# Self edges taken out of a graph kernel's gathers: the edge list compacted on the chip, each window's own rows loaded plainly

## The chip, the cores and the metric

One of the eight cores of a Trainium2 chip runs the whole kernel. The metric is the device time of one execution in microseconds (us). The engines named below are TensorE (PE, its weight loads PEld), VectorE (DVE), ScalarE (ACT), GpSimd (POOL) and SyncE (SP, which here issues DMA transfers and reads registers). Each executes its own instructions in order and waits on semaphores.

## The reference

A graph of 6250 nodes (256 features) has 106250 edges, sorted by destination. 50000 random pairs are there in both directions, and then every node has one edge to itself: each destination has at least one edge, and 6250 of the 106250 edges are such self edges, each the last of its destination. Every edge has one of 8 types.

```python
h = relu(layernorm(x))
for l in range(3):                       # relational layers
    xr  = einsum('nd,rde->rne', h, W_rel[l])
    agg = segment_sum(xr[edge_type, src], dst)
    h   = relu(agg + h @ W_root[l] + bias[l])
x = x + h
h = relu(layernorm(x)); h = h @ Wv + bv  # attention over the same edges
e = leaky_relu(q(h)[src] + k(h)[dst], 0.2)
out = x + segment_sum(h[src] * softmax_by_dst(e), dst)
```

## The kernel before

**Preparation (L517 to L664).** Sources, destinations (twice, the second shifted by one) and types are loaded 128 edges to a row (load_edges, three DMAs each, SP and ACT), turned by PE so that a chunk of 128 consecutive edges is one column (turned, L548), and DVE derives for each of the 831 chunks the node and the (node, type) segment of each edge relative to a window's first node. DVE also checks that the list is sorted and that each window fits; the flag bad_i (L656) selects ordered_path or a general path for other graphs. No instruction of ordered_path starts before the flag. Then x is normalized and written as a table tab[0] in HBM, each row as three bf16 parts whose sum has float32's precision (L688 to L719).

**Windows.** The chunks are grouped into 57 windows (42 of 15 chunks, 14 of 14, a last one of 5). A window covers at most 128 destination nodes from its first node, base, on. For each chunk k of a window, node_ranges gives the nodes that its edges can hit, a range of 13 to 42 nodes; with 8 types that is 104 to 336 segments.

**A relational layer (L908 to L1007).** The loop runs over all chunks (t, k); engine order is as written (manual_schedule). For each chunk: POOL gathers 128 rows of 1536 bytes of tab[l] by the edges' sources (gather, L733), with 30 buffers; DVE makes a one-hot of edges by segments (make_hot, L921), five chunks ahead; PE multiplies message parts by the one-hot into PSUM banks (add, L953, six matmuls, or twelve where the range crosses the middle of the window; with hot_p, also the last chunk of the window before, whose last node can run over). The first half of the banks is copied to ag by ACT when its last chunk is done, the second at the window's end (evacuate, L841). In layer 0 one chunk of each window comes not from the table but from raw rows of x, gathered at the start (L815) and normalized by norm_split.

**The end of a window (finish, L843).** finish is a generator; the loop takes one step of it per chunk of the *next* window. Step 0 turns the window's own rows (xt, loaded by SP at k=1 of the window itself, L994) by six matmuls (L851). Then the output matmuls: 16 products of ag with W_rel (L866) and two with W_root (L870), spread over steps 1 to 12 (to 10 in the last layer) into one PSUM tile po. Then DVE and ACT in turn add the bias and split the result into three parts (L874, L668 to L671), and SP writes them to tab[l + 1] (L878). In the last layer three steps instead add x, normalize, write xa and hx (L893, L903); hx holds 257 columns, the last being the query term. So SP's order in a layer is: xt of window t, write of window t-1 at its end, xt of window t+1.

**Layer ends.** The next layer's gathers need the whole table, so POOL waits there for the last window's write. Weights have two buffers; the load of layer l+1's is issued by ACT at the start of layer l.

**Attention (L1009 to L1097).** Window by window: a gather of 128 hx rows per chunk, logits masked and turned on DVE, ACT and PE, exponentials, and a weighted sum on PE. A window has 16 operands: its chunks and the last chunk of the window before.

## Time and profile before

| what | us |
|---|---|
| median of 10 runs (lowest, highest) | 4349.46 (4347.14, 4352.2) |
| the profiled execution | 4349.26 |
| its span, first to last instruction | 4347.5 |
| POOL: first raw gather; first gather of layer 1, layer 2, attention | 36.2; 1137.7, 2206.6, 3277.0 |
| PE busy, DVE busy, ACT busy, POOL busy | 3731.8, 2123.5, 1269.6, 3165.8 |
| mean clock granted to PE | 0.959 |

Busy time is what an engine spent executing, not issuing. A line of a group names the source line, the engine, the operation, output <- inputs and the count; behind the bar stand busy time and the mean of one in ns, and then the idle time just before, with what ended it. In a table by stretches the columns are the stretch, its length, then for PE, PEld, DVE, ACT, POOL the busy time with the number of instructions, the granted PE clock, the share of the DMA engines and GB/s. A line of a timeline has the start, the length, the instruction and the number of equal ones merged; a bracket gives idle time before it and what ended it. Two lengths may overlap, so starts are compared. SPq means that SP's sequencer issued it.

### The profile page before, as it was taken

What the parts mean: (1) busy time and instruction counts of PE and PEld (TensorE: products, weight loads), DVE (VectorE), ACT (ScalarE), POOL (GpSimd) and SP (SyncE); (2) the same over time, 40 slices, a digit from 0 to 9 for tenths busy, and PEclk for the clock granted to TensorE, in tenths of its full rate; (3) what the DMA queues carried; (4) which work ended last, traced back from release to release, by engine and by line L of the source; (5) the groups of instructions that cost most, each with busy time, mean ns of one, the idle gap of its engine ahead of it and who ended that gap; (6) DMA issues with size and microseconds to landing.
All of it is one profiled execution on the core that took longest, in us unless ns stands there. A gap on an engine that the chain in (4) does not pass through costs nothing. (4 is left out here: it accounts for less than half of the span.)

```text
span 4347.5 us, 85514 instructions
## 1 busy us (share of the span) xinstructions
PE 3731.8 (86%) x31754; PEld 3152.8 (73%) x31754; DVE 2123.5 (49%) x6301; ACT 1269.6 (29%) x2850; POOL 3165.8 (73%) x3403
## 2 busy tenths in 40 slices
PE   0899999999799999999989999999995777777777
PEld 0688888877677777777767777777774666667666
DVE  6444445444333333333334444444445666666665
ACT  5122222222111111111111111111114556555555
POOL 5777777777477777777757777777766777777775
PEclk9999999999999999999999999999997888888888
DMA  6766666666466666666646666666663444444443
GB/s 225 217 180 180 180 180 183 180 180 178 126 180 181 177 180 181 180 180 181 180 142 191 191 188 190 191 191 191 191 175 99 121 120 121 121 121 118 121 123 93
DMA packets 305229, 720.22 MB, mean 166 GB/s; under 512 B 63333, under 2 KB 159409, under 8 KB 304801
## 3 DMA queue, kind: packets, MB, share of 16 engines
q0 software_dynamic: 198608, 596.13, 48.9%
q1 hardware_dynamic: 95868, 109.36, 7.7%
q10 hardware_dynamic: 10324, 9.18, 0.7%
q8 instruction: 251, 4.11, 0.4%
q14 instruction: 178, 1.45, 0.1%
HBM read 660.18 MB, written 54.26 MB: 164 GB/s over the span
## 5 line engine op out<-in xcount | busy, mean ns | idle before, releaser
L733 POOL DMA_INDIRECT msg<-tab,src_t x2436 | 2309.1, 948 | 821.7 <-issue 363.1
L953 PE MATMUL bank<-hot,msg 128*128 128x104 bf16 (+15 forms) x17304 | 1699.5, 241 | 269.4 <-DMA msg<-tab,src_t 164.2
L953 PEld LDWEIGHTS <-msg 128*128 128x128 bf16 x18312 | 1367.2, 98 | 667.2 <-DMA msg<-tab,src_t 292.0
L866 PE MATMUL po<-wr,ag 128*128 128x256 f32 (+1 forms) x5472 | 1537.0, 393 | 44.8 <-DVE hml L671 33.9
L921 DVE TENSOR_SCALAR hot<-up,seg 128x104 bf16<-128x104 f32 (+12 forms) x2493 | 961.5, 430 | 554.8 <-PE bank L953 548.0
L733 POOL DMA_INDIRECT head<-hx,src_t x831 | 787.5, 948 | 280.6 <-issue 94.8
L866 PEld LDWEIGHTS po<-wr,ag 128*128 128x128 f32 (+1 forms) x5472 | 903.2, 190 | 114.4 <-DVE hml L671 39.3
L841 ACT COPY ag<-bank 128x512 f32<-128x512 f32 x675 | 362.0, 589 | 1755.7 <-PE bank L953 1737.7
L874 DVE TENSOR_TENSOR po<-po,bb 128x256 f32<-128x256 f32 x171 | 74.0, 433 | 1016.5 <-PE po L870 1016.5
L1076 PE MATMUL pf<-ex,head 128*128 128x128 f32 (+1 forms) x3548 | 466.9, 295 | 3.3 <-DVE ex L1073 3.2
L1076 PEld LDWEIGHTS pf<-ex,head 128*128 128x128 f32 x3548 | 456.7, 212 | 11.1 <-DVE ex L1073 5.8
L1046 ACT ACTIVATE qm<-other,head 128x128 f32<-128x128 f32 (+1 forms) x887 | 321.3, 398 | 297.9 <-DMA head<-hx,src_t 161.9
L1048 PE MATMUL pq<-ident,qm 128*128 128x128 f32 (+1 forms) x887 | 184.6, 305 | 121.9 <-ACT qm L1046 116.7
L1038 DVE TENSOR_SCALAR other<-up,loc 128x128 f32<-128x128 f32 x831 | 255.8, 341 | 61.9 <-ACT qm L1046 61.3
L1067 PE MATMUL pe<-ident,c 128*128 128x128 f32 (+1 forms) x887 | 152.7, 314 | 123.4 <-ACT c L1061 71.8
L1048 PEld LDWEIGHTS pq<-ident,qm 128*128 128x128 f32 (+1 forms) x887 | 117.7, 149 | 166.7 <-ACT qm L1046 162.3
L1067 PEld LDWEIGHTS pe<-ident,c 128*128 128x128 f32 (+1 forms) x887 | 116.7, 160 | 147.5 <-ACT c L1061 85.6
L1052 DVE TENSOR_REDUCE tops<-pq 128x1 f32<-128x512 f32 (+1 forms) x226 | 153.0, 677 | 123.8 <-ACT c L1051 123.3
L870 PE MATMUL po<-wo,x_t 128*128 128x256 f32 (+1 forms) x684 | 176.4, 380 | 0.0
L1053 DVE SCALAR_TENSOR_TENSOR c<-pq,k_n,c 128x512 f32<-128x512 f32 (+1 forms) x226 | 165.5, 732 | 0.0
L668 ACT ACTIVATE hml<-po 128x256 bf16<-128x256 f32 (+1 forms) x114 | 44.2, 388 | 389.8 <-DVE po L874 362.5
L1051 ACT ACTIVATE c<-pq,sm 128x512 f32<-128x512 f32 (+1 forms) x226 | 145.7, 672 | 2.2 <-DVE sm L1030 1.4
(159 smaller groups left out, 1787.6 us busy)
## 6 DMA issues: line engine op xcount, KB each, us to landing
msg<-tab,src_t POOLq DMA_INDIRECT x2436
xt<-tab SPq DMA_DIRECT2D x168, 192.0 KB
tab<-hml SPq DMA_DIRECT2D x112, 192.0 KB
head<-hx,src_t POOLq DMA_INDIRECT x831
tab<-hml SPq DMA_DIRECT2D x12, 768.0 KB
hx<-row SPq DMA_DIRECT2D x56, 128.5 KB
x<-in_x_dram SPq DMA_DIRECT2D x56, 128.0 KB
xa<-x SPq DMA_DIRECT2D x56, 128.0 KB
```

Of the source, the lines that this page charges most:

```text
L733: nc.gpsimd.indirect_dma_start(out=to, out_offset=None, in_=table[:N, :], in_offset=bass.IndirectOffsetOnAxis(ap=index, axis=0))
L841: nc.scalar.copy(to, of)
L866: nc.tensor.matmul(po[:m], ag[:, h, r, :m], wr[:, h, r, :], start=(r == 0 and h == 0), stop=False, skip_group_check=True)
L870: nc.tensor.matmul(po[:m], x_t[:, h, :m], wo[:, h, :], start=False, stop=(h == KH - 1), skip_group_check=True)
L921: nc.vector.tensor_scalar(hot[:, :R * (hi - lo)], up[:, :R * (hi - lo)], seg[:, i:i + 1], None, op0=ALU.is_equal)
L953: nc.tensor.matmul(banks[b][h][:, a - b * SEG // 2:z - b * SEG // 2], w, hot[:, a - lo:z - lo], start=(not begun[b] and s_ == 0), stop=Fal ...
L1038: nc.vector.tensor_scalar(other[:, :m], up[:, :m], refs[j][1], None, op0=ALU.not_equal)
L1046: nc.scalar.activation(qm[:, :m], other[:, :m], AF.Identity, scale=MASKED, bias=refs[j][0][:, D:HX])
L1048: nc.tensor.transpose(pq[:m, i, :], qm[:, :m], ident)
L1053: nc.vector.scalar_tensor_tensor(to, flat, k1, to, op0=ALU.add, op1=ALU.max)
L1067: nc.tensor.transpose(pe[:, i, :m], c_t[:m, j * P:(j + 1) * P], ident[:m, :m])
L1076: nc.tensor.matmul(pf[:, h, :m], refs[j][0][:, h * P:(h + 1) * P], ex[:, i, :m], start=(j == 0 and h == 0), stop=(j == len(refs) - 1 and h ...
```

## The change

The self edges leave the gathered lists, and 784 chunks take the place of 831: 57 windows again, 51 of 14 chunks, 5 of 13, one of 5.

- Preparation: edges are loaded in overlapping rows of 193 (34 rows for each 4608 edges, 102 rows at a time, 8 times; seven DMAs for each of three arrays, and three for the first nodes). The last edge of each destination is dropped (its word is zero; that it is the self edge is checked for the flag), and its type is noted with the edge before it. Source, node, type and that note are packed in one integer; six steps shift entries left by 1, 2, 4 ... 32 where that bit of the remaining offset is set, each by a mask (into PSUM), a masked copy and a predicated copy. The fields are unpacked and turned. More checks go into the flag.
- Layers: for each window a row tells for every node the type of its self edge (count_loops, computed in layer 0 one window ahead: a one-hot on DVE, a matmul per chunk, a copy). The window's own rows are loaded at k=0, turned at k=3 (own_rows), and by k=7 eight products (one per type) put the own row under the right type in by. evacuate then adds by to the PSUM banks on DVE instead of copying them on ACT. finish loses its step 0's matmuls; its output matmuls take steps 1 to 11 (1 to 9 in the last layer).
- One-hots are made for two chunks by one instruction (make_hots).
- Buffers: messages 26 for 30, weights 1 for 2 (loaded at the start of their own layer), rows 1 for 2, PSUM banks 4 for 5.
- Attention: each window's own 128 rows of hx come as one transfer on SP (mine) and are a further operand; with that a window has 16 operands again.

```diff
--- before.py
+++ after.py
-CW = 15
+
+CW = 14
 LAST = 5
-SPREAD = 4.5
+SPREAD = 4.25
+GR = 36
+GK = 34
+GP = 3
+STEP = 135
+LEAD = 4
+WIDE = 191
+BITS = 6
+OWN = 1024
...
-    NC = -(-E // P)
-    NB = -(-NC // P)
+    NG = E // (GR * P)
+    REST = E - NG * GR * P
+    KR = -(-math.ceil(REST * (1 - N / E) + 4) // P) if REST else 0
+    NC = NG * GK + KR
+    PB = GP * GK
+    NB = -(-NC // PB)
...
+        def load_edges(name: str, a: bass.AP, front: int, fill: int, eng):
+
+            s = prep.tile([PB, NB, WL], I32, name=name)
+            nc.vector.memset(s[:, 0, :LEAD], front)
+            nc.vector.memset(s[:, LB, :], fill)
+
+            def load(to: bass.AP, g: int, i: int, dims):
+                at = a.offset + g * GR * P + i * STEP - LEAD
+                eng.dma_start(to, bass.AP(tensor=a.tensor, offset=at, ap=dims))
+
+            for h in range(GP):
+                nb = (NG - h + GP - 1) // GP
+                b = 0
+                if h == 0:
+                    eng.dma_start(s[0:1, 0, LEAD:], bass.AP(
+                        tensor=a.tensor, offset=a.offset, ap=[[0, 1], [1, WL - LEAD]]))
+                    load(s[1:GK, 0, :], 0, 1, [[STEP, GK - 1], [1, WL]])
+                    b = 1
+                load(s[h * GK:(h + 1) * GK, b:nb, :], b * GP + h, 0,
+                     [[STEP, GK], [GP * GR * P, nb - b], [1, WL]])
+            for i in range(KR):
+                p = NG % GP * GK + i
+                n = min(WL, REST - i * STEP + LEAD)
+                load(s[p:p + 1, LB, :n], NG, i, [[0, 1], [1, n]])
+            return s
...
+        dst_r = load_edges("dst_r", dst, -1, N, nc.sync)
+        src_r = load_edges("src_r", src, -1, N, nc.scalar)
...
+        word = [prep.tile([PB, NB, WIDE], I32, name=f"word{i}") for i in range(2)]
+        nc.vector.scalar_tensor_tensor(word[0], src_r[:, :, :WIDE], 14, tag,
+                                       op0=ALU.logical_shift_left, op1=ALU.bitwise_or)
...
+            n = WIDE
+            for k in range(BITS):
+                a, z = word[k % 2], word[(k + 1) % 2]
+                m = mps.tile([PB, NB, WIDE + 1], I32, name="m")
+                nc.vector.tensor_scalar(m[:, :, :n], a[:, :, :n], 28 - k, 31,
+                                        op0=ALU.logical_shift_left, op1=ALU.arith_shift_right)
+                n1 = n - (1 << k)
+                nc.vector.scalar_tensor_tensor(z[:, :, :n1], m[:, :, :n1], -1, a[:, :, :n1],
+                                               op0=ALU.bitwise_xor, op1=ALU.bitwise_and)
+                nc.vector.copy_predicated(z[:, :, :n1], m[:, :, 1 << k:n], a[:, :, 1 << k:n])
+                n = n1
+            assert n == P
...
-            wp = s.enter_context(tc.tile_pool(name="weights", bufs=2))
-            mp = s.enter_context(tc.tile_pool(name="msgs", bufs=30))
+            wp = s.enter_context(tc.tile_pool(name="weights", bufs=1))
+            mp = s.enter_context(tc.tile_pool(name="msgs", bufs=26))
+            xp = s.enter_context(tc.tile_pool(name="owns", bufs=1))
+            rp = s.enter_context(tc.tile_pool(name="rows", bufs=1))
+            gps = s.enter_context(tc.tile_pool(name="gps", bufs=4, space=PSUM))
...
-            def evacuate(banks, half: int, ag: bass.AP, both: bool):
-
-                for h in range(KH):
-                    to = ag[:, h, :, half * (P // 2):(half + 1) * (P // 2)]
-                    of = banks[half][h].rearrange("p (n r) -> p r n", r=R)
-                    if h and both:
-                        nc.vector.tensor_copy(to, of)
-                    else:
-                        nc.scalar.copy(to, of)
+            def count_loops(t: int):
+
+                n = sizes[t]
+                c0 = first_c[t]
+                width = max(hi - lo for lo, hi in ranges[n])
+                rel = op.tile([P, CW], F32, name="rel")
+                nc.vector.tensor_sub(rel[:, :n], loc[:, c0:c0 + n], lows_n[n])
+                hot = op.tile([P, CW, WMAX // R], BF16, name="hot_n")
+                nc.vector.tensor_tensor(
+                    hot[:, :n, :width], up[:, :width].unsqueeze(1).to_broadcast([P, n, width]),
+                    rel[:, :n].unsqueeze(2).to_broadcast([P, n, width]), ALU.is_equal)
+                yield
+                pl = ops.tile([P, P], F32, name="pl")
+                for k, (lo, hi) in enumerate(ranges[n]):
+                    nc.tensor.matmul(pl[:, lo:hi], own[:, c0 + k:c0 + k + 1].to_broadcast([P, P]),
+                                     hot[:, k, :hi - lo], start=(k == 0), stop=(k == n - 1),
+                                     skip_group_check=True)
+                    if k % 2:
+                        yield
+                nc.scalar.copy(loops[:, t, :spans[n]], pl[:, :spans[n]])
+                yield
...
+            def own_rows(t: int, xt: bass.AP):
                 m = spans[sizes[t]]
+                x_t = rp.tile([P, KH, P], F32, name="x_t", bufs=2)
+                by = xp.tile([P, KH, R, P], F32, name="by")
                 pt = ops.tile([P, KH, P], F32, name="pt")
                 for k in range(KH):
                     for i in range(3):
                         nc.tensor.matmul(pt[:, k, :m], xt[:m, i, k * P:(k + 1) * P],
-                                         ident_b[:m, :m], start=(k == 0 and i == 0), stop=(k == KH - 1 and i == 2),
-                                         skip_group_check=True)
-                x_t = rp.tile([P, KH, P], F32, name="x_t")
+                                         ident_b[:m, :m], start=(k == 0 and i == 0),
+                                         stop=(k == KH - 1 and i == 2), skip_group_check=True)
                 nc.scalar.copy(x_t[:, :, :m], pt[:, :, :m])
+                yield x_t, by
+                for r in range(R):
+                    nc.vector.scalar_tensor_tensor(
+                        by[:, :, r, :m], loops[:, t, :m].unsqueeze(1).to_broadcast([P, KH, m]),
+                        float(r + 1), x_t[:, :, :m], op0=ALU.is_equal, op1=ALU.mult)
+                    if r % 2:
+                        yield x_t, by
+            def evacuate(banks, half: int, ag: bass.AP, by: bass.AP):
+                for h in range(KH):
+                    ns = slice(half * (P // 2), (half + 1) * (P // 2))
+                    nc.vector.tensor_tensor(
+                        ag[:, h, :, ns], banks[half][h].rearrange("p (n r) -> p r n", r=R),
+                        by[:, h, :, ns], ALU.add)
+            def finish(l: int, at, x_t: bass.AP, x0, ag: bass.AP, weights, t: int):
...
+                if last and x0 is None:
+                    x0 = rp.tile([P, D], F32, name="x0")
+                    nc.sync.dma_start(x0, x[ds(at, P), :])
...
-            weights = load_weights(0)
+            for _ in count_loops(0):
+                pass
             for l in range(L):
-                nxt = load_weights(l + 1) if l + 1 < L else load_head()
+                weights = load_weights(l)
+                if l == L - 1:
+                    load_head()
...
+                    pair = op.tile([P, 2, WMAX], BF16, name="hots", bufs=5)
+                    nc.vector.tensor_tensor(
+                        pair[:, :n, :width], up[:, :width].unsqueeze(1).to_broadcast([P, n, width]),
+                        seg[:, i:i + n].unsqueeze(2).to_broadcast([P, n, width]), ALU.is_equal)
...
+                        at = nc.sync.value_load(base_i[0:1, t:t + 1], min_val=0,
+                                                max_val=N - P if t < NW - 1 else N - 1)
+                        m = spans[n]
+                        xt = rp.tile([P, 3, D], BF16, name="xt")
+                        nc.sync.dma_start(xt[:m].rearrange("p s d -> p (s d)"),
+                                          tab[l][ds(at, m), :])
+                        rows_of = own_rows(t, xt)
+                        counts = count_loops(t + 1) if l == 0 and t < NW - 1 else iter(())
...
-                    if i + AHEAD < len(order):
-                        make_hot(i + AHEAD)
+                    if len(hots) < min(i + AHEAD, len(order)):
+                        make_hots()
...
+                    for _ in range(2 if final and k else k >= 3):
+                        x_t, by = next(rows_of, (x_t, by))
                     if 0 in halves and (k == n - 1 or R * ranges[n][k + 1][0] >= SEG // 2):
-                        evacuate(banks, 0, ag, final)
+                        evacuate(banks, 0, ag, by)
                     if k == n - 1 and banks[1] is not None:
-                        evacuate(banks, 1, ag, final)
+                        evacuate(banks, 1, ag, by)
+                    if l == 0:
+                        next(counts, None)
                     for _ in range(-(-STEPS // (n - 1)) if final else 1):
                         while unfinished and next(unfinished[0], "done") == "done":
                             unfinished.pop(0)
...
-                    if k == 1:
-                        at = nc.sync.value_load(base_i[0:1, t:t + 1], min_val=0,
-                                                max_val=N - P if t < NW - 1 else N - 1)
-                        xt = rp.tile([P, 3, D], BF16, name="xt")
-                        m = spans[n]
-                        nc.sync.dma_start(xt[:m].rearrange("p s d -> p (s d)"),
-                                          tab[l][ds(at, m), :])
-                        if l == L - 1:
-                            x0 = rp.tile([P, D], F32, name="x0")
-                            if final:
-                                gather(x0, x, last_c)
-                            else:
-                                nc.sync.dma_start(x0, x[ds(at, P), :])
...
+                mine = rp.tile([P, HX], F32, name="mine")
+                refs.append((mine, lane))
...
+                            nc.sync.dma_start(mine, hx[ds(at, P), :])
```

## The prediction

> **What bounds the kernel now.** I read the page first (engine shares, groups), then busy time by stretches, then the timeline of each engine around one window boundary. The chain that ended last is of no help: it holds only the final output scatter.
>
> ```profile
> PE 3731.8 (86%) x31754; PEld 3152.8 (73%) x31754; DVE 2123.5 (49%) x6301; ACT 1269.6 (29%) x2850; POOL 3165.8 (73%) x3403
> L733 POOL DMA_INDIRECT msg<-tab,src_t x2436 | 2309.1, 948 | 821.7 <-issue 363.1 <-PE bank L953 256.2 <-DMA msg<-tab,src_t 81.0
> L733 POOL DMA_INDIRECT head<-hx,src_t x831 | 787.5, 948 | 280.6 <-issue 94.8 <-PE pf L1076 56.7 <-ACT qm L1046 47.8
> ```
>
> By shares PE looks like the bound. By stretches (layer 0, layer 1, layer 2, attention) POOL shows the same rate everywhere, about 80 gathers in 100 us, whatever the others do:
>
> ```profile
> 300.00:900.00 600.00, 580.04 (x5310) 489.56 (x5308) 295.94 (x854) 143.12 (x342) 454.24 (x479) 1.00 0.63 181
> 1250.00:2100.00 850.00, 789.97 (x7094) 654.66 (x7092) 321.94 (x864) 141.06 (x320) 642.81 (x680) 0.99 0.62 180
> 2350.00:3200.00 850.00, 790.74 (x7114) 661.27 (x7113) 382.13 (x1277) 147.11 (x322) 643.15 (x679) 1.00 0.67 190
> 3400.00:4300.00 900.00, 689.42 (x4782) 616.09 (x4783) 596.21 (x1736) 534.72 (x1203) 681.12 (x719) 0.87 0.44 120
> ```
>
> ```profile
> 1140.19 0.94 POOL L733 DMA_INDIRECT msg<-tab,src_t  x1 [0.30 <-issue]
> 1141.43 0.95 POOL L733 DMA_INDIRECT msg<-tab,src_t  x1 [0.30 <-DMA msg<-tab,src_t]
> 1142.69 0.95 POOL L733 DMA_INDIRECT msg<-tab,src_t  x1 [0.30 <-issue]
> ```
>
> A gather starts every 1.25 us (0.95 and a gap of 0.30, whoever is named). 831 of them are 1039 us: layers 1, 2 and attention are POOL's. A 15-chunk window lasts 15 x 1.25 = 18.75 us there. PE needs less: the layer 0 window from 262.66 to 279.50 has no idle time on PE and is 16.84 us. In layer 0 one gather of each window was made ahead, and PE (967 busy per 1000 us) is as close to the end as POOL; from its first message matmul (123.62) to its last (1118.68) the layer is 995 us.
>
> The place to look at is where a window ends. Layer 1, PE, then DVE, then SP:
>
> ```profile
> 1608.04 1.03 PE L870 MATMUL po<-wo,x_t 128*128 128x256 f32 x4
> 1608.91 1.55 PE L953 MATMUL bank<-hot,msg 128*128 128x264 bf16 x12
> 1610.30 0.30 PE L953 MATMUL bank<-hot_p,msg 128*128 128x8 bf16 x6
> 1610.54 0.45 PE L953 MATMUL bank<-hot,msg 128*128 128x104 bf16 x6
> 1610.83 0.50 PE L851 MATMUL pt<-ident_b,xt 128*128 128x128 bf16 x6
> 1611.56 0.64 PE L866 MATMUL po<-wr,ag 128*128 128x256 f32 x2
> 1615.92 0.67 PE L953 MATMUL bank<-hot,msg 128*128 128x192 bf16 x6 [1.46 <-DMA msg<-tab,src_t]
> ```
>
> ```profile
> 1609.11 0.43 DVE L874 TENSOR_TENSOR po<-po,bb 128x256 f32<-128x256 f32 x1 [5.69 <-PE po L870]
> 1609.99 0.43 DVE L669 SCALAR_TENSOR_TENSOR po<-po,hml 128x256 f32<-128x256 f32 x1 [0.45 <-ACT hml L668]
> 1610.86 0.43 DVE L671 TENSOR_TENSOR hml<-po,hml 128x256 bf16<-128x256 f32 x1 [0.44 <-ACT hml L670]
> ```
>
> ```profile
> 1611.31 0.35 SPq L878 DMA_DIRECT2D tab<-hml  x1
> 1612.49 0.33 SPq L994 DMA_DIRECT2D xt<-tab  x1
> ```
>
> Call T the end of the last L870 (1608.91). The result's split ends at T+2.38, SP issues its table write at T+2.40, and only then, 1.17 later, the load of the next window's own rows xt. SP is in order, so xt is behind the write. The packets on SP's queue show xt landing 3.46 us after its issue (median of 54 windows in each of layers 0 and 1, tenth to ninetieth percentile 2.8 to 4.1). So xt is there at T+7.03. Now nobody cares: it is read a window later.
>
> **The change part by part.**
>
> *Fewer gathers (gain).* 784 chunks for 831: POOL's floor falls by 47 x 1.25 = 59 us in each of four stages.
>
> *PE's work.* A window of 14 chunks has 17760 columns of message matmuls for 19008 (the ranges computed by hand from the formula); 960 more columns cost 0.405 us (the 104 against the 264 rows), so 0.52 us less: 16.84 becomes 16.32. There are 57 windows before and after, so the float matmuls stay.
>
> *Own rows used early (loss, layers 0, 1).* xt is loaded at k=0 and transposed at k=3 of the same window. SP's order is unchanged: write of window t-1, then xt of t+1. PE's order from T, by widths: two last chunks 0.66+0.78, hot_p 0.20, chunks 0 and 1 0.29+0.40, one output pair 0.45, chunk 2 0.44, two pairs 0.90, chunk 3 0.48: it reaches the transposes at T+4.60 and waits for T+7.03. Behind them on PE stand all later chunks; their buffers (26 for 30) come free late, so POOL waits too. The wait does not drift away: T of the next window follows from this one. Cycle: 16.32 + 2.43 = 18.75 us against POOL's 14 x 1.25 = 17.50. Layer 1: 56 x 18.75 + 6 for the short last window = 1056 against 1039: **+17**.
>
> *Copies moved from ACT to DVE.* Four additions of 128x512 out of PSUM a window, at 0.68 (the L839 copy of that shape on DVE; L841 on ACT 0.59). They stand behind the split in DVE's order: from T+2.38 to T+3.65. PE's first output pair wants the first at T+2.33, a wait inside the one above. Eight by-products of 256 elements (0.43 each) run at k=4 to 7 and are wanted at k=9: hidden by about five chunks of PE work, 3.4 us if that cover went. The paired one-hots have as many elements as now in half the instructions: nothing, made five chunks ahead.
>
> *Counting loops, layer 0.* DVE at k=0 now has, in order: the two additions (to T+3.65), statistics 1.08, a pair 0.58, rel 0.10, hot_n of 518 elements 0.74: T+6.17. PE wants hot_n at k=1, T+2.33, before the output pair, so it waits 3.87; the transposes come after that, xt has landed. The 14 counting matmuls: between 0.025 (a hot_p one) and 0.098 (a weight load's mean) each; by width nearest to hot_p, 0.5 us a window. Cycle 16.32 + 0.5 + 3.87 = 20.7; 56 x 20.7 + 8 = 1167 against 995: **+172**.
>
> *Layer 2.* L870 is now at k=9. DVE first makes the half-0 additions (to T+0.55) and a pair with hot_p (0.58), so the chain that put hx<-row at T+4.08 puts it at about T+4.9; xt 1.18 later, landing 3.92 (there x0 follows on the queue): T+10.0. PE is at its transposes at T+6.33. Cycle 16.32 + 3.67 = 20.0; 56 x 20.0 + 6 = 1126 against 1039: **+87**.
>
> *Layer ends.* The last window transposes at k=1: about 2.3 us more wait, three times: **+7**. Single-buffered weights: load issued at the same place as now (1130.11), first read about 29 us later; costed at nothing. Without that cover it is 2.4 MB at 180 GB/s, 13 us a layer.
>
> *Preparation.* No gather starts before the validity flag (POOL's first at 36.19, flag cast at 34.38). The edge loads become 14 issues on ACT's queue and 10 on SP's instead of 6 and 6; the fourth to sixth now take 1.5 to 4 us apiece, so src lands near 23 us rather than 12. After it on DVE, at 1.04 us per 1000 elements (1.08 for 896): word and masks 5; six shift steps of three instructions over 1528 falling to 1024 elements, 25100 elements and 0.1 each on top, 28; fields, turning, bases 14; checks 18: flag at about 88, less what fits in idle time before: **+50**. Bounds 35 (masks at the 0.58 of 830 elements, some checks early) and 70 (loads later). The layer norm (33 to 97 us) then overlaps the 57 raw gathers (72 us), which move by the full 50. Copy_predicated has no row; between 0.52 and 1.04 per element, taken as a two-operand one, 1.04. [...]
>
> *Attention.* 16 operands a window as before, one from SP instead of POOL. ACT waits 129 us of 900 for gathered heads, 14%, more than the 5.7% by which the pace rises: POOL's, **-59**. The 57 loads of mine are read last, some 15 us after issue: nothing.
>
> Sum: 50 + 172 + 17 + 87 + 7 - 59 = **+274** on 4349.26 (span 4347.5 and 1.8 around it; the runs' median is 4349.46): 4623.
>
> [...]
>
> **The rivals.** *xt only:* hot_n isn't on PE's path; layer 0 at 16.32 + 0.5 + 2.35 = 19.2, 1081 us: 4537. For it: DVE is idle half of layer 0. Against: it works in order behind the split.
>
> *POOL stays the bound (faster):* xt lands in time. Layers 1, 2 and attention -59 each, layer 0 56 x 16.82 + 8 = 950, -45, preparation +50: -172, 4177. It needs xt 2.4 us earlier; from 1.25 us earlier layer 1 is POOL's, from 0.3 us earlier it breaks even. For it: with fewer gathers in flight the load may land faster; the lowest tenth is 0.7 faster. Against: SP's order.
>
> *DVE becomes the bound:* preparation 70, half a microsecond more in each of 171 windows, no gain in attention: 4623 + 20 + 86 + 59 = 4788. Against: its work in a layer 0 window comes to 13.5 us of 20.7.
>
> **How the numbers follow.** The forecast's case 0.62: landing times of 2.8 and 4.1 move layers 1 and 2 by 36 us each, preparation by 15 to 20, 4535 to 4720. xt only 0.17, down to 4450 with the fast landing. POOL 0.14, DVE 0.07. Range 4450 to 4720. Under 0.2% (9 us) a measurement of this kernel can't tell from no change; cases near it 0.02. Faster 0.15, slower 0.83.
>
> **What would show it.** In layers 1 and 2 a wait of PE's L851-type transposes on xt once a window, 2 to 4 us, POOL at 72 to 75 gathers per 100 us rather than 80; in layer 0 the counting matmul waiting for hot_n; the first gather at about 86 us; attention still at 1.25 us a gather. Wrong if gathers run at 1.25 us in the layers, or if the transposes never wait.

## The result and the profile after

The changed kernel takes 4937.05 us (median of 8 runs, 4924.54 to 4953.03) where the kernel before takes 4349.1: a ratio of 1.1352, 95% interval 1.1342 to 1.1362. It is slower, as forecast, but by 588 us where the forecast said 274; the time lies 217 us above the upper end of the range.

The profiled execution after has a span of 4928.8 us, 581.3 more than the 4347.5 before. The difference by stretches, each layer from its first to its last matmul into the message banks:

| stretch | before | after | difference | forecast |
|---|---|---|---|---|
| start to first raw gather | 36.2 | 125.1 | +88.9 | +50 |
| to the first message matmul | 87.4 | 83.9 | -3.5 | 0 |
| layer 0 | 995.1 | 1343.6 | +348.5 | +172 |
| layer 1 | 1048.8 | 1096.6 | +47.7 | +17 |
| layer 2 | 1046.9 | 1197.1 | +150.2 | +87 |
| between the layers, to the first gather of attention, and the tail | | | +9.0 | +7 |
| the gathers of attention | 1039.5 | 980.0 | -59.4 | -59 |

Four terms are too small and none has the wrong sign. The stretches of 100 us below show it first (a stretch of layer 0, 1, 2 and of attention; columns as before: PE, PEld, DVE, ACT, POOL busy with instructions, the clock granted to PE, DMA share, GB/s).

```profile
500.00:600.00 100.00, 85.33 (x731) 72.38 (x730) 52.68 (x126) 10.30 (x29) 53.86 (x55) 0.86 0.42 123
2000.00:2100.00 100.00, 89.11 (x827) 75.00 (x826) 56.00 (x123) 6.39 (x17) 70.19 (x75) 1.00 0.58 167
3100.00:3200.00 100.00, 87.92 (x725) 72.63 (x724) 57.95 (x157) 6.33 (x15) 64.32 (x67) 0.91 0.57 161
4300.00:4400.00 100.00, 80.89 (x598) 72.74 (x597) 72.64 (x214) 63.42 (x144) 75.63 (x81) 0.92 0.46 128
```

POOL makes 81 gathers in the stretch of attention, as before, and 55, 75 and 67 in those of the layers, against 80. The page's groups say that it now waits for PE in the layers (935.9 us of idle time before `msg` gathers) and that PE waits for the counting one-hot:

```profile
PE 3952.9 (80%) x32775; PEld 3348.1 (68%) x32775; DVE 2813.8 (57%) x7231; ACT 954.8 (19%) x2248; POOL 3046.2 (62%) x3244
...
L888 POOL DMA_INDIRECT msg<-tab,src_t x2295 | 2233.2, 973 | 1408.8 <-PE bank L1164 935.9
...
L1003 PE MATMUL pl<-hot_n,own 128*128 128x19 bf16 (+9 forms) x784 | 86.7, 187 | 260.4 <-DVE hot_n L997 260.4
```

The window boundary of layer 0 on PE. T is the end of the first row below's four matmuls, 602.85 (the next row on PE starts there):

```profile
601.98 1.03 PE L1062 MATMUL po<-wo,x_t 128*128 128x256 f32 x4
...
604.41 0.83 PE L1164 MATMUL bank<-hots,msg 128*128 128x104 bf16 x12
608.91 0.23 PE L1003 MATMUL pl<-hot_n,own 128*128 128x13 bf16 x2 [3.67 <-DVE hot_n L997]
608.98 1.20 PE L1058 MATMUL po<-wr,ag 128*128 128x256 f32 x2
609.98 1.05 PE L1164 MATMUL bank<-hots,msg 128*128 128x168 bf16 x6
...
615.22 0.66 PE L1164 MATMUL bank<-hots,msg 128*128 128x192 bf16 x6
```

The counting matmul starts at T+6.06 after a wait of 3.67 us; the forecast had T+6.17 and 3.87. But then six matmuls on 168 rows take 1.05 us, and further on the six on 192 rows only 0.66. The stretches of the same boundary carry the reason in the clock column, the third from the end: 1.00, 0.51, 1.00.

```profile
602.00:608.00 6.00, 3.24 (x36) 2.62 (x34) 3.62 (x10) 1.05 (x3) 4.11 (x6) 1.00 0.59 170
608.00:615.00 7.00, 6.09 (x32) 5.08 (x33) 3.05 (x9) 1.19 (x3) 2.41 (x3) 0.51 0.38 121
615.00:626.00 11.00, 11.00 (x107) 9.54 (x106) 6.28 (x15) 0.27 (x1) 6.44 (x7) 1.00 0.36 104
```

PE was granted half its clock there. The trace's clock records put this half rate from 608.17 to 615.00, 6.83 us, and again from 632.07, one window later. In layer 0 there are 56 such stretches with 379 us at half rate; before there was none. Layer 2 has 44 with 154 us, layer 1 has 10 with 34 us (before 3 with 14 us in each of the two).

Layer 1, PE and then SP's queue:

```profile
2037.13 1.03 PE L1062 MATMUL po<-wo,x_t 128*128 128x256 f32 x4
...
2041.08 0.70 PE L1058 MATMUL po<-wr,ag 128*128 128x256 f32 x2 [0.69 <-DVE ag L1036]
...
2044.76 0.51 PE L1020 MATMUL pt<-ident_b,xt 128*128 128x128 bf16 x6 [1.17 <-DMA xt<-tab]
```

```profile
2040.45 0.35 SPq L1070 DMA_DIRECT2D tab<-hml  x1
2041.63 0.33 SPq L1140 DMA_DIRECT2D xt<-tab  x1
```

The load stands behind the table write and is awaited once a window, as forecast; but a wait of 0.69 for the additions (`ag`) comes ahead of it. In layer 2 that wait is longer, and half rate follows it (four output matmuls take 1.99 us there, 1.08 later in the window):

```profile
3170.69 1.57 PE L1058 MATMUL po<-wr,ag 128*128 128x256 f32 x4 [1.75 <-DVE ag L1036]
3172.05 1.05 PE L1164 MATMUL bank<-hots,msg 128*128 128x168 bf16 x6
3172.89 1.99 PE L1058 MATMUL po<-wr,ag 128*128 128x256 f32 x4
...
3175.83 1.08 PE L1058 MATMUL po<-wr,ag 128*128 128x256 f32 x4
```

The preparation, DVE and then ACT's queue. `src` is there at 56.85 us, because six loads of `typ_r` and six of `src_r` stand one after another on ACT's queue, 14.37 and 29.73 us long:

```profile
33.71 1.76 DVE L600 TENSOR_TENSOR dif<-dst_r 102x1536 int32<-102x1536 int32 x1 [16.88 <-DMA dst_r<-in_dst_dram]
...
56.85 1.75 DVE L612 SCALAR_TENSOR_TENSOR word<-src_r,tag 102x1528 int32<-102x1528 int32 x1 [12.21 <-DMA src_r<-in_src_dram]
```

```profile
1.57 14.37 ACTq L547 DMA_DIRECT2D typ_r<-in_edge_type_dram  x6
22.25 29.73 ACTq L547 DMA_DIRECT2D src_r<-in_src_dram  x6
```

One thing is needed to read the later experiments: from the run e8 on the chips gave every kernel, the one before too, a time 22 to 25% longer (5326 to 5422 us for 4350), with idle time put down to issuing (132.6 us ahead of PE's message matmuls in e12, none in the same kernel in e6), so these runs are compared only by their ratio to the kernel before on the same chip and with other runs on that chip.

### The profile page after: what moved, and what is told of

It is laid out like the page before. It is cut to its first block, busy times and chain, and to the rows that moved or that the text cites. A ratio compares the mean times of both kernels' runs of the same rounds, so it can differ in the third digit from the quotient of the medians.

```text
span 4928.8 us, 86747 instructions
## 1 busy us (share of the span) xinstructions
PE 3952.9 (80%) x32775; PEld 3348.1 (68%) x32775; DVE 2813.8 (57%) x7231; ACT 954.8 (19%) x2248; POOL 3046.2 (62%) x3244
## 5 line engine op out<-in xcount | busy, mean ns | idle before, releaser
L888 POOL DMA_INDIRECT msg<-tab,src_t x2295 | 2233.2, 973 | 1408.8 <-PE bank L1164 935.9
L1058 PE MATMUL po<-wr,ag 128*128 128x256 f32 (+1 forms) x5472 | 1690.6, 429 | 144.6 <-DVE ag L1036 130.2
L1164 PE MATMUL bank<-hots,msg 128*128 128x256 bf16 (+14 forms) x17466 | 1672.7, 242 | 68.2 <-DMA msg<-tab,src_t 67.8
L1026 DVE SCALAR_TENSOR_TENSOR by<-loops,x_t 128x256 f32<-128x256 bf16 (+1 forms) x1368 | 485.2, 418 | 620.8 <-ACT x_t L1023 602.1
L1036 DVE TENSOR_TENSOR ag<-bank,by 128x512 f32<-128x512 f32 x678 | 435.5, 684 | 690.8 <-PE bank L1164 690.8
L1119 DVE TENSOR_TENSOR hots<-up,seg 128x304 bf16<-128x304 f32 (+7 forms) x1185 | 694.4, 610 | 1.2 <-PE bank L1164 1.2
L1250 ACT ACTIVATE qm<-other,head 128x128 f32<-128x128 f32 x840 | 293.8, 397 | 193.9 <-DMA head<-hx,src_t 107.9
L1252 PE MATMUL pq<-ident,qm 128*128 128x128 f32 x897 | 180.3, 302 | 115.7 <-ACT qm L1250 106.7
L1241 DVE TENSOR_SCALAR other<-up,loc 128x128 f32<-128x128 f32 (+1 forms) x784 | 239.5, 340 | 31.3 <-ACT qm L1250 31.1
L1271 PE MATMUL pe<-ident,c 128*128 128x128 f32 x897 | 148.0, 305 | 108.3 <-ACT c L1265 64.9
L1252 PEld LDWEIGHTS pq<-ident,qm 128*128 128x128 f32 x897 | 117.8, 148 | 155.3 <-ACT qm L1250 149.3
```

Of the source, the lines that this page charges most:

```text
L888: nc.gpsimd.indirect_dma_start(out=to, out_offset=None, in_=table[:N, :], in_offset=bass.IndirectOffsetOnAxis(ap=index, axis=0))
L1026: nc.vector.scalar_tensor_tensor(by[:, :, r, :m], loops[:, t, :m].unsqueeze(1).to_broadcast([P, KH, m]), float(r + 1), x_t[:, :, :m], op0= ...
L1036: nc.vector.tensor_tensor(ag[:, h, :, ns], banks[half][h].rearrange("p (n r) -> p r n", r=R), by[:, h, :, ns], ALU.add)
L1058: nc.tensor.matmul(po[:m], ag[:, h, r, :m], wr[:, h, r, :], start=(r == 0 and h == 0), stop=False, skip_group_check=True)
L1119: nc.vector.tensor_tensor(pair[:, :n, :width], up[:, :width].unsqueeze(1).to_broadcast([P, n, width]), seg[:, i:i + n].unsqueeze(2).to_bro ...
L1164: nc.tensor.matmul(banks[b][h][:, a - b * SEG // 2:z - b * SEG // 2], w, hot[:, a - lo:z - lo], start=(not begun[b] and s_ == 0), stop=Fal ...
```

## The experiments

Theory: each window of a layer is a chain over PE, DVE and SP, and its waits (for `hot_n` in layer 0, `xt` in layers 1 and 2, `ag` in layer 2) cost their own length and, where PE has stood still long enough, half-rate time after them. The rivals stand in the expectations.

**The changed kernel again (c_after).** No edit.

> The changed kernel as it stands, on the chip of the other runs of this call, so that these can be set against it: about 4937 us, layer 0 1344, layer 1 about 1098. In the three runs so far whose layer 2 has the same code it took 1197, 1229 and 1235 us, so this run is also there to show how far that layer wanders.

4965.28 us, a ratio of 1.142 (1.1392 to 1.1448). Layer 0 took 1341.6, layer 1 1105.2 and layer 2 1228.6. Runs with the same code in layer 2 (the profile after, this one, e2, e3, e4, e7) put it between 1197 and 1236 us; differences of that size in it are not read below.

**Own rows a window earlier (e1).**

```diff
                     if k == 0:
...
-                        xt = rp.tile([P, 3, D], BF16, name="xt")
-                        nc.sync.dma_start(xt[:m].rearrange("p s d -> p (s d)"),
-                                          tab[l][ds(at, m), :])
+                        xt = load_own(t, at) if t == 0 else xt_next
...
+                    if k == 1 and t < NW - 1:
+                        xt_next = load_own(t + 1, nc.sync.value_load(base_i[0:1, t + 1:t + 2], ...))
```

`load_own` holds the three removed lines, with two buffers for `xt`.

> The changed kernel with one edit: the transfer of a window's own rows (xt) is issued a window earlier, at k=1 of the window before, into a second buffer; the rest of the computation stays. Theory 'xt is late': in layer 1 PE's wait for xt (1.17 us in most windows) goes and the window falls from a median of 18.99 to about 17.8 us, the layer from 1097 to about 1005 us; in layer 2 the wait for xt (1.90 in every other window) goes, and with it some of the half-rate time that follows waits, 1197 to about 1090; layer 0 stays within 15 us of 1344, since there the wait for hot_n ends last. Sum: about 4740 us. Rival 'the additions on DVE bind instead': the wait for ag grows by what the wait for xt loses, layers 1 and 2 stay within 20 us and the time is 4900 to 4940.

4770.14 us (1.0959, 1.0941 to 1.0977). The waits for `xt` are gone. Layer 1 fell to 1019.1 (window median 17.44 us, 14 gathers at 1.25: POOL's again), layer 2 to 1117.2, layer 0 stayed (1338.8). The lateness of `xt` is confirmed; it was all of layer 1's loss. In layer 2 the 1.74 us wait for `ag` stayed in nearly every window, each time with 3.41 us at half rate behind it (45 stretches, 154 us), which is why 1090 was not reached.

**Counting later (e2).**

```diff
-                    if l == 0:
+                    if l == 0 and k >= 3:
                         next(counts, None)
```

> The changed kernel with one edit: in layer 0 the steps that count the next window's self edges begin at k=3 and no longer at k=0, so that hot_n and its matmuls stand later in DVE's and PE's order; nothing is left out. Theory 'the 3.67 us wait for hot_n costs itself and the half clock after it': the wait goes, layer 0's wait becomes layer 1's (xt, about 1.2 us), the window falls from 23.88 to about 19.4 us, the layer from 1344 to about 1090, and the 481 us in which the granted clock was 0.50 in layer 0 fall under 60; the whole about 4690 us. Rival 'the half clock comes from what PE computes in layer 0, not from the wait': the wait goes but the half-rate time stays above 400 us, layer 0 at 1200 or more, the whole 4790 to 4850.

4764.91 us (1.0947, 1.0918 to 1.0975). Layer 0 took 1137.2 us, a window 19.64, and the half rate is down to 24 us in 6 stretches. (The 481 us of the expectation count 102 us before the layer's first message matmul too; the layer itself had 379.) What waits in a window is now what waits in layer 1, and half rate hardly ever follows it:

```profile
613.09 0.70 PE L1058 MATMUL po<-wr,ag 128*128 128x256 f32 x2 [0.69 <-DVE ag L1036]
...
616.76 0.51 PE L1020 MATMUL pt<-ident_b,xt 128*128 128x128 bf16 x6 [1.16 <-DMA xt<-tab]
```

The rival is refuted: with the same matmuls in the layer the half rate went when the wait went. The layer lies 47 us above the expected 1090, the median window 0.2 above; the other 28 us over the expected total lie in layer 2 (1232).

**Work put into the wait (e3).** The decisive run: the wait's end stays where it is and PE gets more to do.

```diff
                 pl = ops.tile([P, P], F32, name="pl")
+                for _ in range(40 if t > 0 else 0):
+                    nc.tensor.matmul(pl, ident_b, ident_b, start=True, stop=False,
+                                     skip_group_check=True)
                 for k, (lo, hi) in enumerate(ranges[n]):
```

> The changed kernel with work added: 40 bfloat16 matmuls of 128x128 without use go on PE ahead of the counting matmuls of every window of layer 0, into the bank pl that these then start anew. They need nothing that is late, so they run while PE would wait for hot_n: about 40 x 0.083 = 3.3 us of the 3.67. Theory 'PE falls to half rate because it stood still': hot_n arrives as late as before, but the 6.83 us at 0.50 after it go, so the window falls by about 3.4 us, from 23.88 to about 20.5, layer 0 from 1344 to about 1155, the whole to about 4750 us, with 2240 matmuls more. Rival 'the half rate has another cause': layer 0 stays within 20 us of 1344, or gets longer.

4816.12 us (1.1067, 1.1048 to 1.1085): faster than without the added work. Layer 0 took 1187.6 us, 154 less than the 1341.6 of c_after, and has 6.8 us at half rate in all.

```profile
600.61 2.40 PE L1003 MATMUL pl<-ident_b 128*128 128x128 bf16 x40
604.44 0.20 PE L1006 MATMUL pl<-hot_n,own 128*128 128x13 bf16 x2 [1.43 <-DVE hot_n L997]
604.49 0.68 PE L1061 MATMUL po<-wr,ag 128*128 128x256 f32 x2
605.00 0.60 PE L1167 MATMUL bank<-hots,msg 128*128 128x168 bf16 x6
```

The 40 took 2.40 us (60 ns each, not the 83 assumed), so 1.43 us of wait remain; the counting matmul of the next window starts at T+6.06 as without them. The six matmuls on 168 rows take 0.60 instead of 1.05. A window is 20.96 us for 23.89, so half rate after the wait cost 2.9 us a window.

**Half as much (e7).** `range(20 ...)` for `range(40 ...)`.

> The changed kernel with 20 matmuls without use ahead of the counting ones in layer 0, where 40 left a wait of 1.43 us and no half-rate time: 20 take about 1.2 us, so about 2.6 us of the 3.67 stay. It tells how long PE may stand still. If it takes about 3 us of standing still, as the 2.9 us between the start of the wait and the start of the half rate in the changed kernel suggest: no half rate, layer 0 about 1190 and the whole about 4815, as with 40. If 1.75 us are enough, as layer 2's wait for ag suggests: half rate in most windows, layer 0 1300 or more, the whole above 4900.

4839.72 us (1.1129, 1.1111 to 1.1148), layer 0 1218.9: between the two. One such wait:

```profile
614.80 0.20 PE L1006 MATMUL pl<-hot_n,own 128*128 128x13 bf16 x2 [2.54 <-DVE hot_n L997]
```

After a wait of that length half rate came in 19 of 56 windows, 78 us. So no length of wait decides alone. Inside the layers of the changed kernel the half-rate stretches are 3.41 or 6.83 us long, and the distances between their starts are multiples of 3.41 (7 of them, 23.89, in layer 0; most often 6, 20.48, in layer 2): the half rate began and ended on a grid of 3.41 us. PE was not idle for all of a piece of this grid before it: in layer 2 waits of 1.75 us were enough. With the grid laid on the ten traces up to e7 (before, after, c_after, e1 to e7), the pieces of 3.41 us at full rate in the layers show where the limit lies: where PE's busy time in the profile was under 40% of a piece, half rate followed in all 433; from 40 to 50% in 292 of 395; from 50 to 60% in 9 of 317; above that in 2 of 8004. So in these traces the clock was halved after a piece in which PE was busy for less than about half of it. Layer 2's wait of 1.75 us is half of 3.41, and half rate followed it in 44 windows of 57; the wait of 2.54 us in e7 was followed by half rate wherever 1.99 us or more of it fell into one piece, and never where at most 1.7 us did.

**Edge loads on 32 partitions (e4).**

```diff
-                load(s[h * GK:(h + 1) * GK, b:nb, :], b * GP + h, 0,
-                     [[STEP, GK], [GP * GR * P, nb - b], [1, WL]])
+                for p0, p1 in ((0, 32), (32, GK)):
+                    load(s[h * GK + p0:h * GK + p1, b:nb, :], b * GP + h, p0,
+                         [[STEP, p1 - p0], [GP * GR * P, nb - b], [1, WL]])
```

and the same for the 33 rows of the first block.

> The changed kernel with one edit: each load of edges onto 34 (or 33) partitions is split into one of 32 and one of 2 (or 1), twelve transfers more; nothing is left out. [...] Rival 'the time goes into the packets (772 bytes each) or into issuing on one queue': twelve more transfers on the same queues, and the first raw gather comes no earlier, or up to 10 us later.

The first raw gather came at 100.9 us for 125.1. The ten loads of `src_r` now take 10.74 us where six took 29.73, and the words are made at 28.32:

```profile
1.56 9.62 ACTq L547 DMA_DIRECT2D typ_r<-in_edge_type_dram  x10
12.48 10.74 ACTq L547 DMA_DIRECT2D src_r<-in_src_dram  x10
```

```profile
28.32 1.73 DVE L614 SCALAR_TENSOR_TENSOR word<-src_r,tag 102x1528 int32<-102x1528 int32 x1
```

The whole took 4938.27 us (1.1345, 1.1326 to 1.1364), since layer 2 fell on 1235.5 in this run. The arrangement of the loads is the cause of the late `src`, and the rival falls: the same bytes, rows of the same 772 bytes, more transfers, a third of the time. In the changed kernel the 16 DMA engines were busy to 0.1 or 0.2 in nearly every slice of the first 28 us, while the loads of `typ_r` and `dst_r` ran; after that loads of x ran beside those of `src_r`. With the split loads of `typ_r` and `dst_r` they were busy to 0.2 to 0.8 in the slices from 2 to 12 us. Over how many engines a load of 34 partitions went is not shown.

**Three edits together (e5: e1, e2 and e4).**

> The changed kernel with three edits together: xt a window early, the counting from k=3 on, the edge loads split into 32 and 2. Theory 'each named wait costs itself and what half clock follows it, and nothing stands behind them': layer 0 loses both waits and its window falls to PE's own 17.4 to 17.8 us, the layer to about 1000; layer 1 about 1015 and layer 2 about 1115 as with the early xt alone; first raw gather 101; the whole about 4400 us, so the change would still not be faster than the 4350 before. Rival 'DVE comes next': the additions of the two halves hold the output products back in layer 0 as well, the window stays above 19 us and the whole above 4480.

4508.46 us (1.0358, 1.0341 to 1.0375). Layer 1 (1019.6), layer 2 (1111.4) and the first gather (100.8) are as expected, layer 0 is not: 1109.9 us, a window 19.57. The rival holds, what is next is DVE's order:

```profile
611.58 0.70 PE L1060 MATMUL po<-wr,ag 128*128 128x256 f32 x2 [0.69 <-DVE ag L1038]
...
616.69 0.21 PE L1005 MATMUL pl<-hot_n,own 128*128 128x13 bf16 x2 [1.28 <-DVE hot_n L999]
```

**Output products over fewer chunks (e6: e5 and this).**

```diff
-                parts = STEPS - (4 if last else 2)
+                parts = STEPS - (6 if last else 4)
```

> The three edits together and a fourth: the output products of a window are spread over two chunks fewer (7 for 9 steps in layer 2, 9 for 11 in layers 0 and 1), so that the result's own chain on DVE is over before the additions of the second half are due. Theory 'what is left in layer 2 is the 1.75 us wait for ag behind that chain, and the half clock after it': layer 2 falls from about 1115 to about 1000 us, layers 0 and 1 by 0 to 30; the whole about 4280 us, faster than the 4350 before. Rival 'packing the output products more closely only moves the wait': layer 2 stays above 1080, the whole above 4370.

4357.28 us, the kernel before 4350.77 beside it: a ratio of 1.0016 (1.0007 to 1.0026). Four edits that move nothing but the order and the form of transfers took back nearly all of the 588 us. Layer 0 took 1017.3 us (93 less where 0 to 30 were expected: `ag` is there in time, and `hot_n` 0.25 us late), layer 1 1001.6, layer 2 1063.5 with 37 us at half rate.

```profile
500.00:600.00 100.00, 97.87 (x937) 82.32 (x936) 71.75 (x176) 13.86 (x42) 74.95 (x77) 1.00 0.62 176
1700.00:1800.00 100.00, 94.52 (x870) 80.22 (x869) 59.22 (x133) 6.38 (x17) 75.93 (x80) 1.00 0.64 180
2700.00:2800.00 100.00, 92.08 (x832) 79.06 (x833) 64.61 (x174) 6.71 (x16) 76.01 (x79) 1.00 0.69 190
```

POOL is at 77 to 80 gathers a stretch, and the clock at 1.00 in all three. In layer 2 a wait of 1.53 us for `ag` is left in nearly every window, followed by half rate in 11. Neither expectation came true there: 1000 was not reached and 1080 (the rival) undercut, and the whole lies between their 4280 and 4370.

**Products a chunk later, flags in SBUF (e8, e10, e11, e14: e6 and these).**

```diff
                 yield
+                yield
-                parts = STEPS - (6 if last else 4)
+                parts = STEPS - (8 if last else 6)
...
-                m = mps.tile([PB, NB, WIDE + 1], I32, name="m")
+                m = prep.tile([PB, NB, WIDE + 1], I32, name="m")
```

> The four edits together and two more. First, the output products of a window start a chunk later (k=2 for k=1) and are spread over 5 chunks in layer 2 and 7 in layers 0 and 1 (7 and 9 so far). Theory 'the additions of the second half stand behind the result's chain in DVE's order': in layer 2 the chain is over about 1.2 us earlier and the products ask 0.6 us later, so the 1.53 us wait for ag goes, and the layer falls from 1064 to about 1000 us; layers 0 and 1 by 0 to 15. Rival 'the additions wait for the banks, not for the chain': layer 2 stays above 1050. Second, the flags m of the compaction lie in SBUF and no longer in PSUM: the six shifts that make them should take 0.95 instead of 1.74 us, as the shift 'some' of the same 1528 integers does, so the first raw gather comes about 4.7 us earlier, 96 us for 100.6; if the memory of the output makes no difference, 100.6. The whole about 4285 us, 1.5% below the 4350 before.

> The same six edits as in the run e8, again, because the chip of that run was slow throughout (the kernel before took 5414 us there, 4350 elsewhere). What the run is to tell is as before: layer 2 from 1064 to about 1000 us if the additions stood behind the result's chain, above 1050 if they wait for the banks; first raw gather at about 96.5 us, where it came even on the slow chip, against 100.6 with the flags in PSUM; the whole about 4285 us.

> The six edits once more, since the chips of the last two runs of them gave every kernel, the one before too, a time 22 to 25% longer, in the attention's gathers as well (1.69 and 1.64 us apiece for 1.25), so that layer 2 could not be set against that of the four edits. On a chip where the kernel before takes 4350: layer 2 about 1000 us if the additions stood behind the result's chain, above 1050 if they wait for the banks; the whole about 4285.

> The four edits again on the same chip, as the measure for the run beside it: layer 2 about 1064 us and the whole about 4357 where the kernel before takes 4350.

Beside all four runs of these edits, and the repetition of the four edits (e12), the kernel before took 5326 to 5418 us, so none of them can be set against e6 directly. Ratios to the kernel before: e8 0.9788 (0.9758 to 0.9818), e10 0.975 (0.9725 to 0.9775), e11 0.976 (0.9737 to 0.9782), e14 0.9775 (0.975 to 0.98), and the four edits e12 0.9792 (0.9773 to 0.9811). On their common chip the intervals of e11 and e12 overlap, so a gain of the whole from these edits isn't shown. On the chip of e11 and e12, layer 2 took 1230.1 with and 1263.3 without the later start, layer 0 1167.3 and 1148.8. In e11 the wait for `ag` is no longer among PE's seven largest, and one for `hot_p`, which DVE makes behind the same additions, has taken its place; first e12, then e11:

```profile
PE po L1060 <- DVE ag L1038: 150.5, 102, 4.5
```

```profile
PE bank L1175 <- DVE hot_p L1118: 136.2, 84, 3.1
```

That fits additions that stand behind DVE's other work, with the wait moved to the next item of DVE's order; the expected times (1000 or above 1050) could not be put to the test, so it stays open.

The flags are settled: the first raw gather came at 96.5, 96.0 and 96.2 us for 100.6 (and 100.5 in e12 on e11's chip). The six shifts into PSUM had a median of 1703 ns in the changed kernel (first row), into SBUF 924 in e11 (second):

```profile
L635 DVE TENSOR_SCALAR m<-word x6: 1476/1703/1752, 67.8 to 96.7; 102x1528 int32<-102x1528 int32 x1, 102x1520 int32<-102x1520 int32 x1, 102x1504 int32<-102x1504 int32 x1, 102x1472 int32<-102x1472 int32 x1
```

```profile
L637 DVE TENSOR_SCALAR m<-word x6: 807/924/943, 38.8 to 68.5; 102x1528 int32<-102x1528 int32 x1, 102x1520 int32<-102x1520 int32 x1, 102x1504 int32<-102x1504 int32 x1, 102x1472 int32<-102x1472 int32 x1
```

Copy_predicated stayed the same (1776 and 1790 ns), with the flags in either memory.

**Types on POOL's queue (e9: e8 and this).**

```diff
-        typ_r = load_edges("typ_r", edge_type, 0, 0, nc.scalar)
+        typ_r = load_edges("typ_r", edge_type, 0, 0, nc.gpsimd)
```

> As the run before it, with the loads of the edge types issued on POOL's queue and no longer on ACT's ahead of those of the sources. If the arrival of the sources still sets the compaction's start, its first word comes some 8 us earlier and the first raw gather 3 to 8 us earlier; if DVE's own work sets it (DVE is busy from 14 us on), the gather stays within 2 us. The layers are the same.

0.9784 (0.9751 to 0.9818), and the first gather at 98.6 us, 2.2 later than in e8, just outside what either case allowed. The loads of `src_r` were issued by 14.3 us (22.2 in e8), yet the first word came at 39.48 for 28.19, since DVE's instructions stood in another order and DVE was at work on others until then. So it wasn't the arrival of `src` that set the word's time here; what an earlier arrival alone is worth isn't shown.

**The later start for layer 2 alone (e13, e15).**

```diff
                 yield
+                if last:
+                    yield
-                parts = STEPS - (6 if last else 4)
+                parts = STEPS - (8 if last else 4)
```

with the flags in SBUF as in e8.

> The six edits with one taken back for layers 0 and 1: only layer 2's output products start a chunk later and take 5 chunks; layers 0 and 1 keep k=1 and 9 chunks as with the four edits (beside each other on a slow chip the later start cost layer 0 18 us: 1167 for 1149). On a chip where the kernel before takes 4350: layer 0 1017 and layer 1 1002 as with the four edits, layer 2 about 1000 if its additions stood behind the result's chain and above 1050 if they wait for their banks; first raw gather 96.5; the whole about 4290. Where the chip is slow throughout, the ratio to the kernel before is below the 0.976 of the six edits.

> The six edits as in e8, e10 and e11, beside the run before it: layer 2 the same as there; if the later start costs layers 0 and 1 something on any chip, these are 5 to 18 us longer here each.

> The edits of e13 once more, for their time where the kernel before takes 4350 us: layers 0 and 1 at 1017 and 1002 us as with the four edits, layer 2 about 1000 if its additions stood behind the result's chain and above 1050 if they wait for their banks, first raw gather 96, the whole about 4290. On a chip slow throughout: a ratio near e13's 0.973.

Ratios of 0.9727 (0.9693 to 0.9761) and 0.9717 (0.97 to 0.9733), the lowest of all, though the interval of e13 overlaps that of e14 beside it; on that chip layer 0 took 1163.7 (e13) and 1181.0 (e14), layer 2 1249.6 and 1250.7. Where the kernel before takes 5418 or 5422 us, the changed kernel with its order put right is thus 2.8% faster; where that one takes 4350 the best measured is e6, which is no faster, and e13 was not seen there.

## Why the prediction was wrong, and where it was right

*Fewer gathers; attention.* Right: -59.4 for -59, 1.25 us a gather before and after.

*Counting loops, layer 0: the step that failed.* The wait itself was right to 0.2 us (it ends at T+6.06 for T+6.17 and lasts 3.67 for 3.87; the forecast's own T+6.17 less T+2.33 would be 3.84). The step that failed is the sum after it, "Cycle 16.32 + 0.5 + 3.87 = 20.7", which took the cycle as work plus wait, with every matmul at its usual length. Instead the wait of 3.67 us put PE at half rate for 6.83 us, from 0.74 us before the wait's end on, and the cycle was 23.89; e3, with the wait's end unchanged and no half rate, gives the forecast's cycle nearly as worked out: 20.96 us for 20.7, 1187.6 us for 1167. The other 156 us of the layer, half of the whole miss of 307, are clock. The profile of before hardly showed it: three stretches with 14 us in each of layers 1 and 2 and none in layer 0, where PE had no such wait in each window.

*Layer 2.* Of the mechanism a part was right: `xt` landed at T+9.98 (`hx` issued at T+4.33, `xt` 1.18 later, landing 4.47) for T+10.0, with some luck, since `hx` was 0.6 us earlier than forecast and the landing 0.55 longer. Missing were the wait for `ag`, 1.75 us, and the same half rate after it (154 us; four output matmuls took 1.99 us in it and 1.08 after it): the forecast gave the additions only "a wait inside the one above", that for `xt`, but in layer 2 those of the second half stand behind statistics, shift and scores in DVE's order. Early `xt` took back about 110 us (1229 in c_after to 1117), closer products another 48.

*Own rows, layer 1.* Right in mechanism, +47.7 for +17: PE goes on with the transposes at T+6.98 (median) for T+7.03. That this fits so well is partly luck: the last packet of `xt` came 2.84 us after the issue (median) and not 3.46, but PE went on only 3.26 after it. Mis-sized was PE's own part. In a window PE waits 2.08 us (median; 0.69 for `ag`, 1.34 for `xt`) for 2.43, but without its waits it takes 16.93 us and not 16.32: the 0.52 us that fewer columns were to save from 16.84 did not show. The rest is the mean window, 19.31 for the median of 18.99, with the ten half-rate stretches in it.

*Preparation.* +89 for +50. DVE's part from `src` to the flag came out as forecast, 56.85 to 122.77 or 66 us for 88 - 23 = 65, but partly by luck: 11 us of DVE's work on the edges were done before `src` came, and 11 us of the layer norm stood in between. Wrong was `src` at 23 us: the loads were priced at 1.5 to 4 us apiece like rows of other shapes. Split into 32 and 2 partitions they gave back 24 of the 39 us. The price of the six mask shifts, 1.04 us per 1000 elements like the other two instructions of each step and so about 9 of the forecast's 28 us, was right: they took 10.0 us with the flags in PSUM, and moving them to SBUF brought the first gather 4 to 4.6 us earlier.

*Copies moved from ACT to DVE.* The price was right (1.28 for two additions), the cover was not: PE waits 0.69 for the first of them in layer 1, and in layer 0 where `hot_n` is out of the way (e2). Where `xt` and `hot_n` were out of the way (e5), this wait set the pace together with the moved `hot_n`, and packing the products closer (e6) removed 93 us from layer 0.

*The rivals.* "xt only" fell: `hot_n` is on PE's path. "POOL stays the bound" fell for the kernel as it is; e1 and e6 show that it needed what its text said, an earlier `xt`, and in layer 0 also a later `hot_n` and earlier additions. "DVE becomes the bound" fell in the form given (attention gained in full, DVE busy 57%); but as an order in which items come late, DVE is where the waits for `hot_n` and `ag` come from.

*The range.* Its upper end took in landing times and the preparation. No case had a wait lengthen the work after it, so no end could reach 4937.

## What to carry to other kernels

When a change adds a wait of 1.5 us or more to every turn of a loop on PE (here half rate followed 1.53 us in 11 windows of layer 2 in e6 and 1.75 us in 44 of 57 after the change), price the matmuls after it at half rate as a separate case: here 3.67 us of waiting cost 6.6, 2.9 of them by half rate. Ask of each item that a change adds to an in-order engine what stands behind it in each turn; taking the item out of the way of the bound engine (an earlier load, a later one-hot, closer products) gave back 580 of 588 us without removing any work. A load onto 34 partitions was slow enough to be split: 32 and 2 took a third of the time (10.74 us for 29.73).

## What was not expected of the hardware

- Half rate came after waits well below the 2.9 us that lay between the start of layer 0's wait and the start of its half rate: after 1.75 us in layer 2 (44 windows of 57), 1.53 in 11 windows (e6), 1.16 with 0.69 hardly ever (6 stretches in layer 0 of e2), 2.54 in a third of the windows (19 of 56, e7). In the layers of the changed kernel it lasted 3.41 or 6.83 us. What told them apart was PE's busy share in one piece of the 3.41 us grid: half rate followed 292 of 395 pieces at 40 to 50%, and 9 of 317 at 50 to 60%.
- The grid of 3.41 us held a loop: with half rate in each window, windows of layer 0 lasted 23.89 us, seven times 3.41, almost without spread (23.38 to 24.12, but for the last), also where the own rows came a window earlier.
- Work without use made the kernel faster by 2.5 to 3% (4816 for the 4937 and 4965 without).
- The four edits stand at 1.0016 of the kernel before where that one takes 4350 us, and at 0.9792 where it takes 5326. Fewer gathers may be why; no run tells.
